# A graph network's first layer: its products placed behind every third group of edge counts in place of every second

## The chip, the cores and the metric

The kernel runs on one core of one Trainium2 chip, as one program in one launch. The metric is the device time of one execution in microseconds (us); below it is given as the median of 14 runs, and one more execution was profiled.

## What is computed

Four graph layers run one after the other over 6250 nodes with 128 features and 206250 edges (src, dst, weight), sorted by dst. Ahead of each stands a layer norm with ReLU, and each adds its result to x. Cut to what matters here, layer 0 and the shape of the rest:

```python
h = relu(layernorm(x))
neighbor = segment_sum(edge_weight[:, None] * h[src], dst, 6250)       # layer 0
x = x + leaky_relu(neighbor @ W1.T + b1 + (h * neighbor) @ W2.T + b2, 0.2)
h = relu(layernorm(x))
x = x + graph_norm_layer(h, segment_sum(h[src], dst) / degree)         # layer 1
x = x + clique_layer(relu(layernorm(x)))                               # layer 2: means of x_clique rows, one linear map
x = x + gru_layer(relu(layernorm(x)))                                  # layer 3: sums of messages, GRU gates, one linear map
```

## The kernel before

Instead of gathering rows by edge, the kernel builds dense matrices. The nodes are cut into 49 blocks of 128. For every destination node it counts, by source node, how many edges there are (`cnt`, small integers) and how large the sum of their weights is (`edge_w`). Layer 0 multiplies by `edge_w` as soon as it is there. The counts go to DRAM, straight (`cnt_d`) and turned by DMA transposes (`cntT_d`), and layers 1 to 3 read them in a second stage (`dense`, line 1023), which the change doesn't touch.

**Strips.** The first stage takes 25 strips of 256 destination nodes (two blocks; the last strip has one). In a strip, two nodes share the 128 partitions as two halves of 64 (`WN` = 2, `H` = 64): a partition holds one edge of a node. Four such pairs of nodes (`PW` = 4) make one **count**, so a strip has 32 counts, numbered 0 to 31 below, and the last strip 16.

**A count** (`count`, line 769) is 24 bf16 matmuls on PE (line 784) of one-hot matrices: `s_hot` (which node within a source block) as weights, `k_hot` (which block, and the same times the three parts of the edge's weight) as moving operand. They write a PSUM tile `pK` of two banks. ACT then copies it out twice: cast to 8-bit integers into `cnt` (line 793), and a copy into `edge_w` (line 791). The pool `banks` has three such tiles (line 606), and the tag `pK` is shared: the transposes `pt` and `pv` and the products `po` and `pf` named below each take one of the three in turn as well.

**One-hots** (`one_hots`, line 750) are made by DVE for four counts at a time (`TW` = 16): `s_hot` (line 762) and `k_hot` (lines 764 and 765). There are two sets. At the first count of a group of four, the set for the next group is put into DVE's queue; it overwrites the set of the group before.

**The products of layer 0** (`layer0`, line 813) for strip k are made while strip k+1 is counted: 49 source blocks, for each of them one fp32 matmul by each half of the partitions, into `pB` and `pM` (line 821; each runs as two instructions, so a source block is two steps of a pair). `layer0` is a generator: each call of `next(before)` issues one **visit** of some source blocks and stops. Before the change there are 16 visits, each of three source blocks but for the last with four. After the last visit ACT and DVE add `pB` and `pM` into `agg` (lines 829 and 830), and `finish0` (line 845) is queued as the **ends** of that strip.

**Ends and keys** come at fixed places too. `finish0` is a generator that is visited before the counts 2, 6, 10, 14, 18, 22 and 30 of the following strip (`END_AT`, piece by piece; four counts are a piece): the transposes `pt` of h (line 842) with DVE's product `inter` (line 851), then the products `po` (lines 858 and 859) with the sums and statistics on DVE, then the norm's steps on ACT and DVE, a second `pt` before count 22 that ACT copies to `ht`, and `pf` (line 879) before count 30. The keys of the next strip are prepared by `prepare` (line 667), begun behind count 27 of the strip before and visited before the counts 2, 10, 14, 22 and 26 (`EDGES_AT`): offsets on DVE (lines 683 to 705, then 714 to 705), indirect fetches of edges by POOL (line 642), the split of the weights in three on POOL (lines 586 to 589), and before count 26 five transposes `pv` on PE (line 739), which ACT copies out as `keys` and `by_edge` (line 744).

The whole order is written by hand: the stage stands under a manual schedule, and what is issued first in Python stands first in each engine's queue. `strip` (line 940) lays it down. For each count: a new set of one-hots if a group begins; the visits for ends and keys if the count is the third of its piece; the count; a visit of the products if the count's number is odd (lines 962 and 963); and after the last count of a piece the DMA transposes of `turn`, on SP's queue. So a visit for ends and keys always stands right behind a visit of the products.

Of the kernel before, what the change touches and what calls it, by code (L numbers as in the profile page):

```python
# [464 lines left out]
WN = 2  # L465
H = P // WN
SB = 2
SW = SB * P
STRIPS = [(k, min(SB, NB - k * SB)) for k in range(-(-NB // SB))]
NS = len(STRIPS)  # L470
TW = 16
TI = 2
PW = 4
# [26 lines left out]
def fast(ctx: ExitStack, tc: tile.TileContext, a: dict, out: bass.AP, flag: bass.AP):  # L500
# [41 lines left out]
    def flat(t):  # L542
        return t.rearrange("p b f -> p (b f)")
# [55 lines left out]
    with ExitStack() as bx:  # L599
# [150 lines left out]
        def one_hots(by_edge, t0):  # L750

            of = slice(t0 // TI, t0 // TI + tq)
            keys, parts = (t[:, of, :, None, :] for t in by_edge)

            def at(i, n):
                return keys[:, :, i].to_broadcast([P, tq, n, TI])

            def count_up(n):
                return iota[:, None, :n, :].to_broadcast([P, tq, n, TI])

            s_hot = hot.tile([P, tq, P, TI], BF16, name="s_hot")
            nc.vector.tensor_tensor(s_hot, count_up(P), at(0, P), op=ALU.is_equal)  # L762
            k_hot = hot.tile([P, tq, 4, NBP, TI], BF16, name="k_hot")
            nc.vector.tensor_tensor(k_hot[:, :, 0], count_up(NBP), at(1, NBP), op=ALU.is_equal)  # L764
            nc.vector.tensor_tensor(k_hot[:, :, 1:, :NB], k_hot[:, :, :1, :NB].to_broadcast([P, tq, 3, NB, TI]),  # L765
                                    parts.to_broadcast([P, tq, 3, NB, TI]), op=ALU.mult)
            return s_hot, k_hot

        def count(w0, hots, cnt, edge_w):

            s_hot, k_hot = hots

            pk = banks.tile([P, WN, 512], F32, name="pK")
            for i in range(PW):
                (u, t), o = divmod(w0 % TW + i, TI), 2 * NBP * i
                for j in (0, 2, 3):
                    for h in range(WN):
                        r = slice(h * H, (h + 1) * H)
                        if j:
                            to, rhs = slice(o + NBP, o + NBP + NB), k_hot[r, u, j, :NB, t]  # L780
                        else:
                            both = k_hot[r, u, :2, :, t].rearrange("p j b -> p (j b)")
                            to, rhs = slice(o, o + NBP + NB), both[:, : NBP + NB]
                        nc.tensor.matmul(pk[:, h, to], s_hot[r, u, :, t], rhs, start=j == 0,  # L784
                                         stop=True, skip_group_check=True)
            by_block = pk[:, :, : 2 * PW * NBP].rearrange("p h (i c b) -> p c b i h", c=2, b=NBP)
            n0, nn = w0 * WN, PW * WN
            pairs = flat(cnt).bitcast(U8).rearrange("p (b n e) -> p b e n", n=P, e=2)
            for j, m in enumerate((pairs[:, :, :, n0 % P : n0 % P + nn], edge_w[:, :, n0 : n0 + nn])):
                if j:  # L790
                    nc.scalar.copy(m.rearrange("p b (i h) -> p b i h", h=WN), by_block[:, 1, :NB])  # L791
                else:
                    nc.scalar.copy(m.rearrange("p b e (i h) -> p b e i h", h=WN),  # L793
                                   by_block[:, 0].rearrange("p (b e) i h -> p b e i h", e=2))

        def turn():


            kept = None
            for g in range(NQB):  # L800
                c, i = CHUNK_OF[g]
                for q in range(0, NPR, KP):
                    tt = turned.tile([P, KP, P], U16, name="tt")
                    nc.sync.dma_start_transpose(tt, cnt_d[c, :, i, q * P : (q + KP) * P])
                    if kept:
                        nc.sync.dma_start(*kept)
                    kept = cntT_d[:, g, q * P : (q + KP) * P], flat(tt)
                    yield
            nc.sync.dma_start(*kept)

        turns0 = SW // (WN * PW * 2)

        def layer0(k, nb, edge_w):

            g, w = k * SB, nb * P
            pl = [psum.tile([P, 512], F32, name=n) for n in ("pB", "pM")]
            for i in range(turns0):
                for s in range(i * NB // turns0, (i + 1) * NB // turns0):
                    for h in range(WN):
                        r = slice(h * H, (h + 1) * H)  # L820
                        nc.tensor.matmul(pl[h][:, :w], h0[r, s, :], edge_w[r, s, :w], start=s == 0,  # L821
                                         stop=s == NB - 1)
                if i + 1 < turns0:
                    yield
            if k == NS - 1:
                ends.append(pl)
                return
            agg = work.tile([P, SW], F32, name="agg")
            nc.scalar.copy(agg[:, :w], pl[0][:, :w])
            nc.vector.tensor_add(agg[:, :w], agg[:, :w], pl[1][:, :w])  # L830
            ends.append(finish0(g, nb, agg))
# [99 lines left out]
        before, ends, turns, edges = iter(()), [], turn(), prepare(1)  # L931
# [8 lines left out]
        def strip(k, nb):  # L940
            nonlocal before, edges, by_edge, hots
            edge_w = edge[k % 2].tile([P, NB, SW], F32, name="edge_w")
            end = ends.pop() if ends else iter(())
            last, piece, following = nb * P // WN, 0, None
            for w0 in range(0, last, PW):
                if w0 % TW == 0:
                    now, t1 = hots, w0 + TW
                    if t1 < last:
                        hots = one_hots(by_edge, t1)
                    elif following:  # L950
                        hots = one_hots(following, 0)
                if w0 // PW % PT == PT // 2:
                    if piece in END_AT:
                        next(end, None)
                    if piece in (EDGES_AT if k else FIRST_AT):
                        following = next(edges, None)
                if w0 // PW % 2 and piece in (NORMS_AT[k] if k < 2 else ()):
                    next(norming, None)
                if w0 * WN % P == 0:
                    cnt = cnts.tile([P, NPR, P], U16, name="cnt")  # L960
                count(w0, now, cnt, edge_w)
                if k and w0 // PW % 2:
                    next(before, None)
                g, w1 = k * SB + w0 * WN // P, w0 + PW
                if w1 * WN % P == 0:
                    c, i = CHUNK_OF[g]
                    nc.sync.dma_start(cnt_d[c, :, i, :], flat(cnt))
                if w1 % (PW * PT) and w1 < last:
                    continue
                if piece == NEXT_AT and k + 2 < NS:  # L970
                    edges = prepare(k + 2)
                    next(edges)
                for _ in range(TURN_AT.count(piece) if k else 0):
                    next(turns, None)
                piece += 1
            by_edge = following
            for _ in before:
                next(end, None)
            for _ in end:
                pass  # L980
            before = layer0(k, nb, edge_w)

        def found_all():

# [5 lines left out]
            nc.vector.tensor_copy(flag, p_all)  # L990

        strip(*STRIPS[0])
        nc.vector.tensor_add(b12, b12, b2)
        for k, nb in STRIPS[1:-1]:
            strip(k, nb)
        total = found_all()
        next(total)
        strip(*STRIPS[-1])
        end = ends.pop()
        pt = banks.tile([P, WN, 512], F32, name="pt", tag="pK")  # L1000
# [525 lines left out]
def gnn_kernel(tc: tile.TileContext, a: dict, out: bass.AP):  # L1526
    nc = tc.nc
    with tc.tile_pool(name="flag", bufs=1) as keep:
        flag = keep.tile([1, 1], I32, name="flag")
        fast(tc, a, out, flag)  # L1530
        found = nc.values_load(flag[0:1, 0:1], min_val=0, max_val=2 * E,
                               skip_runtime_bounds_check_because="a count of edges, each at most twice")
        with tc.If(found != E):
            general(tc, a, out)
# [48 lines left out]
```

## Time and profile before

| | |
|---|---|
| median of 14 runs | 1844.3 us (1842.52 to 1845.45) |
| the profiled execution | 1843.03 us |
| its span, first to last instruction | 1841.2 us |
| granted TensorE clock, mean | 0.990 |
| first strip begins to count at | 31.3 us |
| second strip | 71.4 us |
| third strip | 111.5 us |
| the last strip (25th) | 955.9 us |
| the dense layers begin at | 1001 us |
| DVE's busy time per strip (529.6 to 567.8) | 33.9 of 38.2 us |
| ACT's busy time per strip (the same) | 28.8 of 38.2 us |

Engines are PE (matmul), PEld (weight load, beside PE), DVE, ACT, POOL and SP, which issues DMAs. Times are us from the start of the span. In a row of the timeline stand start, duration, engine, line, operation, output<-input with their shapes and the number of instructions merged (x48); where the engine stood idle before, the idle time and what ended it follow in brackets. Matmuls are pipelined: a row's duration is longer than the distance to the next start, and it is the distance that PE's queue pays. Shown durations are rounded to 0.01 us. In the list of waits stand the waiting engine and line, what it waited for, the total, the number of waits and the longest.

### The profile page before, as it was taken

The page shows a single profiled execution, that of the slowest core. Times are in us where ns is not written, and L with a number is a line of the kernel's source. Part 1 is how long each engine was busy: PE and PEld are TensorE (multiplying, and loading weights), DVE is VectorE, ACT ScalarE, POOL GpSimd, SP SyncE. Part 2 cuts the span into 40 slices and gives each one's busy share as a digit, 9 for nine tenths or more (in the row PEclk, how much of TensorE's full clock was granted, in tenths as well). Part 3 has the DMA queues.
Part 4 walks back from the last instruction along what each step waited for, and adds up shares of the span by engine and source line. Part 5 has one row for each costly group of instructions (what it writes and reads, how often), then busy time and mean ns, then how long its engine had stood idle before and what let it go on. Part 6 is the DMA issues. An engine that isn't in the chain of part 4 may idle for free. (4 is left out here: it accounts for less than half of the span.)

```text
span 1841.2 us, 65339 instructions
## 1 busy us (share of the span) xinstructions
PE 1777.7 (97%) x28191; PEld 1511.7 (82%) x28191; DVE 1392.3 (76%) x2946; ACT 1203.7 (65%) x2835; POOL 474.0 (26%) x431
## 2 busy tenths in 40 slices
PE   2799999999999999999999999999999999999997
PEld 2698888888888888888888888888888877787776
DVE  7888888888888888888886777777777854444543
ACT  5777777777777777777774777777556653443442
POOL 2433334333334333343323012111122200000000
PEclk9799999999999999999999999999999999999999
DMA  4255554544535555454214555554555544344442
GB/s 106 57 123 119 127 124 100 140 117 124 121 100 133 112 124 121 100 132 114 83 56 152 163 172 170 166 152 125 147 148 149 154 134 152 109 149 137 133 131 61
DMA packets 262514, 231.73 MB, mean 126 GB/s; under 512 B 101518, under 2 KB 246424, under 8 KB 262215
## 3 DMA queue, kind: packets, MB, share of 16 engines
q1 hardware_dynamic: 253415, 210.67, 42.6%
q0 software_dynamic: 8800, 16.78, 3.3%
q8 instruction: 223, 3.65, 0.8%
q14 instruction: 76, 0.62, 0.1%
HBM read 130.37 MB, written 76.54 MB: 112 GB/s over the span
## 5 line engine op out<-in xcount | busy, mean ns | idle before, releaser
L821 PE MATMUL pB<-edge_w,h 64*128 64x256 f32 (+1 forms) x2450 | 613.1, 385 | 1.0 <-issue 0.7
L821 PE MATMUL pM<-edge_w,h 64*128 64x256 f32 (+1 forms) x2450 | 613.2, 385 | 0.0
L1086 PE MATMUL acc<-wide,parts 128*128 128x512 f32 (+2 forms) x2548 | 574.1, 383 | 2.7 <-DVE wide L1064 1.3
L1086 PEld LDWEIGHTS acc<-wide,parts 128*128 128x128 f32 x2548 | 460.3, 188 | 100.8 <-issue 10.5
L793 ACT CAST cnt<-pK 128x400 uint8<-128x400 f32 x784 | 397.6, 507 | 192.8 <-PE pK L784 175.7
L821 PEld LDWEIGHTS pB<-edge_w,h 64*128 64x128 f32 x2450 | 422.2, 187 | 34.9 <-issue 1.3
L784 PEld LDWEIGHTS <-s_hot 64*128 64x128 bf16 x18816 | 379.4, 95 | 70.9 <-issue 18.0
L821 PEld LDWEIGHTS pM<-edge_w,h 64*128 64x128 f32 x2450 | 422.0, 187 | 0.4 <-DVE flag L990 0.2
L784 PE MATMUL pK<-k_hot,s_hot 64*128 64x49 bf16 (+1 forms) x18816 | 396.6, 192 | 25.3 <-ACT edge_w L791 11.4
L791 ACT COPY edge_w<-pK 128x392 f32<-128x392 f32 x784 | 400.8, 511 | 0.0
L765 DVE TENSOR_TENSOR k_hot<-k_hot,by_edge 128x2352 bf16<-128x2352 bf16 x196 | 272.3, 1389 | 8.5
L762 DVE TENSOR_TENSOR s_hot<-iota,keys 128x2048 bf16<-128x2048 bf16 x196 | 239.3, 1221 | 43.5 <-PE pK L784 41.5
L1064 DVE TENSOR_SCALAR_CACHE_REDUCE wide<-ring 128x512 fp32r<-128x512 uint8 (+2 forms) x325 | 193.3, 650 | 25.4 <-issue 15.9
L1062 ACT ACTIVATE wide<-ring 128x512 fp32r<-128x512 uint8 (+2 forms) x312 | 184.7, 595 | 24.3 <-ACT wide L1062 19.6
L642 POOL DMA_INDIRECT dst<-in_dst,off_i x50 | 84.8, 1696 | 378.9 <-DVE node L705 369.4
L1056 ACT CAST wide<-ring 128x1024 fp32r<-128x1024 uint8 (+3 forms) x130 | 120.7, 957 | 71.0 <-PE acc L1086 68.2
L1055 DVE CAST wide<-ring 128x1536 fp32r<-128x1536 uint8 (+2 forms) x130 | 119.6, 945 | 53.3 <-PE acc L1086 41.2
L1086 PE MATMUL acc<-wide,q_parts 128*128 128x512 f32 (+2 forms) x650 | 157.4, 392 | 1.2 <-DVE wide L1041 1.2
L1086 PEld LDWEIGHTS acc<-wide,q_parts 128*128 128x128 f32 x650 | 115.6, 188 | 28.2 <-DVE wide L1041 2.9
L764 DVE TENSOR_TENSOR k_hot<-iota,keys 128x800 bf16<-128x800 bf16 x196 | 125.9, 642 | 0.0
L1427 POOL DMA_DIRECT2D out<-x x12 | 10.2, 851 | 322.9 <-DVE x L1424 293.1
L642 POOL DMA_INDIRECT src<-in_src,off_i x50 | 78.0, 1561 | 15.2 <-issue 15.2
(246 smaller groups left out, 1610.6 us busy)
## 6 DMA issues: line engine op xcount, KB each, us to landing
ring<-cnt_d SPq DMA_DIRECT2D x110, 640.0 KB, 4.5
cnt_d<-cnt SPq DMA_DIRECT2D x49, 800.0 KB, 4.5
cntT_d<-tt SPq DMA_DIRECT2D x125, 160.0 KB, 3.5
ring<-cntT_d SPq DMA_DIRECT2D x60, 320.0 KB, 3.1
ring<-cnt_d SPq DMA_DIRECT2D x10, 480.0 KB, 3.5
ring<-cnt_d SPq DMA_DIRECT2D x10, 320.0 KB
h<-in_x SPq DMA_DIRECT2D x12, 256.0 KB, 4.4
xs<-in_x SPq DMA_DIRECT2D x24, 128.0 KB, 3.8
```

Of the source, the lines that this page charges most:

```text
L642: nc.gpsimd.indirect_dma_start(out=t, out_offset=None, in_=col[name], in_offset=bass.IndirectOffsetOnAxis(ap=idx, axis=0))
L762: nc.vector.tensor_tensor(s_hot, count_up(P), at(0, P), op=ALU.is_equal)
L764: nc.vector.tensor_tensor(k_hot[:, :, 0], count_up(NBP), at(1, NBP), op=ALU.is_equal)
L765: nc.vector.tensor_tensor(k_hot[:, :, 1:, :NB], k_hot[:, :, :1, :NB].to_broadcast([P, tq, 3, NB, TI]), parts.to_broadcast([P, tq, 3, NB, T ...
L784: nc.tensor.matmul(pk[:, h, to], s_hot[r, u, :, t], rhs, start=j == 0, stop=True, skip_group_check=True)
L791: nc.scalar.copy(m.rearrange("p b (i h) -> p b i h", h=WN), by_block[:, 1, :NB])
L793: nc.scalar.copy(m.rearrange("p b e (i h) -> p b e i h", h=WN), by_block[:, 0].rearrange("p (b e) i h -> p b e i h", e=2))
L821: nc.tensor.matmul(pl[h][:, :w], h0[r, s, :], edge_w[r, s, :w], start=s == 0, stop=s == NB - 1)
L1056: nc.scalar.copy(to[:, 3:ks], of[:, 3:ks])
L1062: one = nc.scalar.activation(to[:, k], of[:, k], AF.Copy, accum_out=total)
L1064: one = nc.vector.tensor_scalar(to[:, k], of[:, k], 1.0, None, op0=ALU.mult, op1=ALU.add, accum_out=total)
L1086: nc.tensor.matmul(acc[:, : nb * P], parts[:, s, j, :], rhs, start=s + j == 0, stop=s == end and j == 1)
```

## The change

The products get a visit after every third count of a strip in place of every second, and after the last count. The number of visits is set to match: 32 counts over 3, rounded up, are 11, so that a visit has four or five source blocks (4, 4, 5, 4, 5, 4, 5, 4, 5, 4, 5). They stand behind the counts 2, 5, 8, 11, 14, 17, 20, 23, 26, 29 and 31. In the last strip of 16 counts there are six (2, 5, 8, 11, 14, 15) for the strip before it, and the other five follow behind the counts. The products of the last strip itself keep 16 pieces. All instructions stay, and their sizes; ends and keys stay before the counts at which they stood. Which visits of ends and keys stand right behind products does change: those before the counts 6, 18 and 30 do, the others stand between two counts.

```diff
-        turns0 = SW // (WN * PW * 2)
-
-        def layer0(k, nb, edge_w):
+        every = 3
+        turns0 = -(-SW // (WN * PW) // every)
+
+        def layer0(k, nb, edge_w, turns0):
...
                 count(w0, now, cnt, edge_w)
-                if k and w0 // PW % 2:
+                if k and (w0 // PW % every == every - 1 or w0 + PW == last):
                     next(before, None)
...
-            before = layer0(k, nb, edge_w)
+            before = layer0(k, nb, edge_w, turns0 if k < NS - 1 else SW // (WN * PW * 2))
```

In this text a line number is that of the kernel before; from line 812 on the changed kernel's are one higher.

## Prediction

> **What bounds the kernel now.** I read the page first, then busy time by stretches, then who waited for whom, then single stretches of the timeline.
>
> The busy line of the page, and the table of stretches for the third strip (starts at 111.5) and for one in the middle (columns: stretch; its length; busy us of PE, PEld, DVE, ACT, POOL; granted clock; DMA):
>
> ```profile
> PE 1777.7 (97%) x28191; PEld 1511.7 (82%) x28191; DVE 1392.3 (76%) x2946; ACT 1203.7 (65%) x2835; POOL 474.0 (26%) x431
> ```
> ```profile
> 111.50:149.70 38.20, 38.20 (x993) 33.84 (x991) 33.47 (x60) 28.82 (x71) 14.67 (x12) 1.00 0.45 118
> 529.60:567.80 38.20, 38.20 (x992) 33.84 (x990) 33.86 (x61) 28.81 (x72) 14.53 (x13) 1.00 0.48 119
> ```
>
> PE is busy in all of a strip's 38.20 us; DVE in 33.9, ACT in 28.8. From 111 to 950 the list of waits has for PE only:
>
> ```profile
> PE pK L784 <- issue: 1.6, 2, 0.9
> PE pB L821 <- issue: 0.7, 2, 0.4
> ```
>
> So in layer 0 time is what PE's queue holds, in order, and any new wait of PE is lost. Twenty-two strips (the 3rd to the 24th) run alike, 38.21 us each but for four of 39.0 to 39.3.
>
> **What a visit costs.** One pair of counts and one visit, on PE:
>
> ```profile
> 543.91 0.95 PE L784 MATMUL pK<-k_hot,s_hot 64*128 64x99 bf16 x48
> 544.70 0.46 PE L821 MATMUL pB<-edge_w,h 64*128 64x256 f32 x1
> ...
> 545.00 0.38 PE L821 MATMUL pB<-edge_w,h 64*128 64x256 f32 x1
> ...
> 545.22 0.38 PE L821 MATMUL pB<-edge_w,h 64*128 64x256 f32 x1
> ...
> 546.08 0.31 PE L784 MATMUL pK<-k_hot,s_hot 64*128 64x99 bf16 x8
> ```
>
> Two counts take 0.79 (0.40 each). The first products of a visit take 0.30 until the next start, all others 0.216, so a visit costs 0.08 beside its products, and a source block (two such steps) 0.432. Blocks stay 49 per strip; visits fall from 16 to 11: 5 x 0.08 = **-0.41 per strip**. A visit becomes 1.81 (four blocks) or 2.24 (five). That is the whole gain on PE, except that the transposes of line 739 now follow a count and no longer a product (0.31 until they start, against 0.21 within a visit): -0.09.
>
> **What the counts then meet.** A count writes one of three buffers in turn (tag pK), shared with the transposes (pt, pv) and products (po, pf) of the visits for ends and keys. In the second strip, where ACT is late, the rule can be read (ACT, then PE):
>
> ```profile
> 77.38 0.48 ACT L791 COPY edge_w<-pK 128x392 f32<-128x392 f32 x1
> ...
> 78.14 0.50 ACT L791 COPY edge_w<-pK 128x392 f32<-128x392 f32 x1
> ```
> ```profile
> 77.91 0.57 PE L784 MATMUL pK<-k_hot,s_hot 64*128 64x99 bf16 x24 [0.74 <-ACT edge_w L791]
> 78.69 0.57 PE L784 MATMUL pK<-k_hot,s_hot 64*128 64x99 bf16 x24 [0.20 <-ACT edge_w L791]
> ```
>
> 77.38 + 0.48 = 77.86 and 78.14 + 0.50 = 78.64: each count starts 0.05 after a copy ends; counted through, it is the copy of the count three before it. How late that copy is with ACT at rest, for the pair at 543.91:
>
> ```profile
> 544.51 0.49 ACT L793 CAST cnt<-pK 128x400 uint8<-128x400 f32 x1 [0.51 <-PE pK L784]
> 544.90 0.49 ACT L791 COPY edge_w<-pK 128x392 f32<-128x392 f32 x1
> ```
>
> Cast 0.60 after the count's start, copy done at 545.39, so its buffer comes back 1.53 after the count began. Two counts and a visit take 2.2: hidden today, since every visit for ends or keys stands right behind a product visit (counts 2, 6, 10 ... behind counts 1, 5, 9 ...). With thirds, products stand behind counts 2, 5, 8, ..., 29 and 31. The visits before counts 6 and 30 still follow one. Three that use a buffer do not: before count 2 (pt), 22 (pt), 26 (pv).
>
> T is us from count 0.
>
> - Count 2 comes third after count 0 (0, 1, pt, 2). It arrives at 0.80 + 0.12 (four transposes, as from 520.93 to 521.05) = 0.92. ACT first copies agg (533.79 to 534.17, count 0 at 533.59), casts at 534.24, has copied at 535.12: buffer back at T = 1.53 + 0.05 = 1.58. **+0.66**. The transposes lose 0.30 there today (1.22 from 535.77 to 536.98, less 0.80 of counts, less 0.12) in the order of PE's two halves; that falls under this wait: **-0.30**.
> - Count 4 needs pt's buffer, freed by DVE's product L851. DVE today:
>
> ```profile
> 536.27 1.38 DVE L765 TENSOR_TENSOR k_hot<-k_hot,by_edge 128x2352 bf16<-128x2352 bf16 x1
> 537.58 0.41 DVE L851 TENSOR_TENSOR inter<-agg,pt 128x256 f32<-128x256 f32 x1
> ```
>
>   Its chain (agg, one-hots, L851) starts with the strip and is not moved: done at 537.99, T = 4.40, plus 0.05. PE arrives at 1.58 + 0.40 + 1.81 + 0.40 = 4.19: **+0.26** (today it arrives at 4.67).
> - Count 23 comes third after count 21 (21, pt, 22, 23): arrives 0.92 after count 21's start, may start after 1.53: **+0.62**.
> - Count 26 comes third after count 24 (24, 25, pv, 26): 0.80 + 0.385 (pv, 563.70 to 564.09) = 1.19 against 1.53: +0.35. But pv also waits for POOL:
>
> ```profile
> 547.77 0.14 DVE L705 TENSOR_SCALAR node<-f_node 128x1 f32<-128x1 f32 x1
> ```
> ```profile
> 562.63 0.63 POOL L589 TENSOR_TENSOR vals<-rest,vals 128x128 bf16<-128x128 f32 x1
> ```
>
>   POOL's fetches and splits end at 563.27, 15.4 after L705, whose place on DVE hardly moves (T = 14.4): vals come at 29.8. PE reaches pv at T = 29.1 (with the waits above; today 30.1), its last transpose can start at 29.85, count 26 at 30.0. **+0.49** in all.
>
> Sum per strip: -0.41 - 0.09 - 0.30 + 0.66 + 0.26 + 0.62 + 0.49 = **+1.23**, so 39.44.
>
> One-hots: DVE may start a set when the group of four counts two back has been counted, and needs 3.13 (551.52 to 554.65) after 0.20 of latency. Between the end of count 15 and count 20 there are four counts and one four-block visit, 1.6 + 1.81 = 3.41: 0.2 + 3.13 + 0.05 = 3.38 just fits. Elsewhere there is a second visit, or line 858's products (1.09), as cover; the margin at count 8 is 0.6. If that cover goes, PE waits once per strip. ACT has 0.77 x 3 = 2.3 of copies per 3.2 and the same other work; SP's and POOL's transfers keep their places and get a longer strip.
>
> The other strips: no product visits in the first. The second has no ends, and ACT, with the norms' work, is behind in half of it; -0.4 + 0.5 (pv) + a bound of 1 either way: +0.3. The last (16 counts, one block): the waits at counts 2 and 4 less two visits, +0.66 + 0.26 - 0.30 - 0.16 = +0.5. The dense layers after 1001 us aren't touched.
>
> 22 x 1.23 + 0.3 + 0.5 = 27.9. The profiled execution took 1843.0 (span 1841.2 and 1.8 around it): 1843.0 + 27.9 = 1870.9. The median of the runs is 1844.3, 1.3 above the profiled one: **1872**.
>
> **Bounds.** Low: no wait at count 4, pv only by its bank, -0.80 + 0.62 + 0.62 + 0.35 = +0.79, x 22 = 17.4, 1862. High: pv 0.3 later and the one-hots of count 20 late by 0.36 (L573 and L575, which stand ahead of them, 550.86 to 551.22), +1.9, x 22 = 42, 1886.
>
> **A rule that speaks against the change.** Short waits left the clock alone here: PE had 1.8 us of gaps in the second strip's first half, single ones up to 0.74, at clock 1.00; the clock had been 0.50 in a stretch after one wait of 4.9 us (47.2 to 52.1).
>
> ```profile
> 74.20:91.80 17.60, 15.82 (x418) 13.77 (x414) 15.01 (x49) 15.11 (x41) 6.04 (x5) 1.00 0.24 38
> 50.30:57.10 6.80, 4.27 (x131) 3.91 (x132) 4.66 (x10) 6.79 (x19) 4.92 (x4) 0.50 0.34 129
> ```
>
> The Trainium skill ("TensorE: Matmul & The Clock Gate", "A second HAM failure mode: psum-queue depth-cycling") warns that PE, idling briefly between groups of matmuls as it cycles PSUM banks, can swing between full and half clock. By it, with that page's window of 3.4 us at half clock once a strip, an estimate would add 22 x 1.7 = 37 us. The sum goes by the row: nothing.
>
> **Rivals.**
> 1. *Waits as worked out*: 1872, own range 1862 to 1882. 70%.
> 2. *DVE or POOL fall behind too*: the one-hots' margin of 0.03 goes, or pv comes later: 1882 to 1895. For: 33.9 of 38.2 us DVE busy. Against: the strip grows by 1.2, which gives DVE time. 15%.
> 3. *Waits partly hidden*: one of the two waits for ACT does not come; +0.3 to +0.7 per strip, 1850 to 1862. 7%.
> 4. *Faster*: the count behind pt or pv finds its buffer free, so that only the visits' starts change: 23 x (-0.41 - 0.09) = -11.5, 1833. The place is the buffer of the count two before pt; it decides if that comes back within 0.92 of the count's start. Against: 1.53 in the rows. 5%.
> 5. *Gain and waits cancel*, within 0.2% (about what a measurement of this kernel can tell from no change): 3%. That the edit does nothing is out: on PE the same instructions stand in another order, products behind every third count.
>
> Faster 0.05 (case 4), same 0.03 (5), slower 0.92. The range 1858 to 1886 takes case 1, some half of 2 and the top of 3.
>
> **What would show it.** Right: strips of 39.4; PE waits in L784 with ACT edge_w as releaser, some 1.3 us a strip, before the third and the 24th count; a smaller one for DVE inter, one at pv for POOL vals; first products of a visit still 0.30, 11 per strip; clock 1.00. Wrong: strips under 38.2 with no wait at those counts (case 4); L784 waiting for k_hot L765 at count 20 (case 2); a clock below 1.00.

## The result, and the profile after

| | before | after |
|---|---|---|
| median | 1844.3 us (28 runs, 1842.38 to 1845.45) | 1865.98 us (6 runs, 1864.92 to 1867.37) |
| ratio, 95% interval | | 1.0118 [1.0108, 1.0128] |
| profiled execution, its span | 1843.03, 1841.2 us | 1866.88, 1865.1 us |
| second, third, last strip begin | 71.4, 111.5, 955.9 us | 71.3, 112.8, 979.2 us |
| a strip with no other pause | 38.21 us | 39.29 us |

Slower by 1.2%, as predicted (1872, with a range of 1858 to 1886). On two occasions the kernel before itself took some 1868 us instead of some 1845, for reasons that stay open, so the kernels run on one of those occasions are compared only with one another.

The busy line of the page after, and the table of stretches for two strips (fourth and fourteenth; columns as before):

```profile
PE 1773.2 (95%) x28191; PEld 1514.5 (81%) x28191; DVE 1405.6 (75%) x2946; ACT 1190.5 (64%) x2835; POOL 474.5 (25%) x431
```
```profile
152.61:191.89 39.28, 38.10 (x991) 34.03 (x989) 34.14 (x60) 28.24 (x71) 14.98 (x13) 1.00 0.56 122
546.15:585.45 39.30, 38.16 (x991) 34.22 (x989) 34.32 (x60) 28.24 (x71) 14.60 (x12) 1.00 0.49 114
```

PE had no gap in 38.20 us before; now it is busy for 38.1 of 39.3, with ACT and DVE about as busy as before. The clock is still 1.00. The list of waits of PE from 112 to 975 names what came in:

```profile
PE pK L784 <- ACT edge_w L791: 22.5, 60, 0.7
PE pv L739 <- POOL vals L589: 1.4, 3, 0.5
PE pK L784 <- issue: 0.3, 1, 0.3
PE pB L822 <- issue: 0.2, 1, 0.2
```

Sixty waits for ACT's copy where there was none. (The list counts idle time after the modelled end of the matmul before, so its figures are lower than the distances between starts, which are what PE loses.) They stand before the counts 2, 23 and 26, three to a strip, except in strips where PE was late there anyway. A fourth wait, before count 4, is too short for the list: PE loses 0.25 there, but the idle time left of it is about 0.1. It shows in the starts. DVE and PE in the fourteenth strip (count 0 at 546.15):

```profile
550.13 0.41 DVE L852 TENSOR_TENSOR inter<-agg,pt 128x256 f32<-128x256 f32 x1
```
```profile
547.73 0.57 PE L784 MATMUL pK<-k_hot,s_hot 64*128 64x99 bf16 x24 [0.46 <-ACT edge_w L791]
549.94 1.63 PE L784 MATMUL pK<-k_hot,s_hot 64*128 64x99 bf16 x72
```

The first row of PE is count 2, the second holds the counts 3, 4 and 5. DVE is done with the buffer of `pt` at 550.13 + 0.41 = 550.54, and count 4 starts at 550.60; over the 22 strips it starts 0.05 behind the end of that row (median), as predicted.

The wait before count 23 in the timeline, PE and then ACT:

```profile
570.75 0.55 PE L784 MATMUL pK<-k_hot,s_hot 64*128 64x99 bf16 x24
571.14 0.31 PE L843 MATMUL pt<-f_ident,h 64*128 64x64 f32 x4
571.29 0.56 PE L784 MATMUL pK<-k_hot,s_hot 64*128 64x99 bf16 x24
572.27 0.57 PE L784 MATMUL pK<-k_hot,s_hot 64*128 64x99 bf16 x24 [0.42 <-ACT edge_w L791]
```
```profile
571.34 0.49 ACT L793 CAST cnt<-pK 128x400 uint8<-128x400 f32 x1 [0.89 <-PE pK L784]
571.73 0.49 ACT L791 COPY edge_w<-pK 128x392 f32<-128x392 f32 x1
```

Count 21 starts at 570.75, the transposes follow, then count 22; ACT has copied count 21 at 571.73 + 0.49 = 572.22, and count 23 starts 0.05 later, 1.52 after count 21. Without the wait it would have started 0.40 behind count 22, at 571.69: 0.58 lost. ACT had stood idle for 0.89 before it: it isn't ACT's load that delays, but the two operations in a row that free the buffer, behind a count of 0.40.

### The profile page after: what moved, and what is told of

Same layout as the page of the kernel before. It is cut to its first block, busy times and chain, and to the rows that moved or that the text cites. A ratio compares the mean times of both kernels' runs of the same rounds, so it can differ in the third digit from the quotient of the medians.

```text
span 1865.1 us, 65362 instructions
## 1 busy us (share of the span) xinstructions
PE 1773.2 (95%) x28191; PEld 1514.5 (81%) x28191; DVE 1405.6 (75%) x2946; ACT 1190.5 (64%) x2835; POOL 474.5 (25%) x431
## 4 chain that ended last, share of the span: by engine, by line
PE 80%; DVE 9%; ACT 3%; issue 3%; DMA 2%; POOL 2%; POOLq 0%; DVEq 0%; ACTq 0%
PE acc L1087 35%; PE pB L822 22%; PE pK L784 13%; DVE k_hot L765 2%; DVE s_hot L762 2%; ACT cnt L793 1%; DMA wgt<-in_edge_weight,off_i 1%; PE pA L1231 1%; PE pM L822 1%; ACT edge_w L791 1%; DVE k_hot L764 1%; PE pf L880 1%; PE po L859 1%; PE pM L1378 1%; PE pA L1423 1%
## 5 line engine op out<-in xcount | busy, mean ns | idle before, releaser
L822 PE MATMUL pB<-edge_w,h 64*128 64x256 f32 (+1 forms) x2450 | 583.5, 381 | 0.4 <-ACT agg L830 0.3
L822 PE MATMUL pM<-edge_w,h 64*128 64x256 f32 (+1 forms) x2450 | 583.2, 381 | 0.0
L793 ACT CAST cnt<-pK 128x400 uint8<-128x400 f32 x784 | 405.7, 517 | 238.2 <-PE pK L784 236.2
L822 PEld LDWEIGHTS pB<-edge_w,h 64*128 64x128 f32 x2450 | 430.9, 187 | 35.8 <-ACT agg L830 0.4
L784 PEld LDWEIGHTS <-s_hot 64*128 64x128 bf16 x18816 | 369.3, 95 | 98.4 <-issue 51.5
L784 PE MATMUL pK<-k_hot,s_hot 64*128 64x49 bf16 (+1 forms) x18816 | 386.0, 192 | 53.0 <-ACT edge_w L791 38.5
L822 PEld LDWEIGHTS pM<-edge_w,h 64*128 64x128 f32 x2450 | 430.8, 187 | 1.2 <-DVE flag L991 0.2
L791 ACT COPY edge_w<-pK 128x392 f32<-128x392 f32 x784 | 409.0, 522 | 0.0
L762 DVE TENSOR_TENSOR s_hot<-iota,keys 128x2048 bf16<-128x2048 bf16 x196 | 251.5, 1283 | 39.7 <-PE pK L784 37.5
L1406 DVE SCALAR_TENSOR_TENSOR wb<-pT,f_b_hh,wb 128x512 f32<-128x512 f32 (+1 forms) x12 | 8.9, 740 | 91.1 <-PE pT L1403 91.1
```

## Experiments

Theory A is that of the prediction: a count finds its buffer occupied when it comes third after a count that began less than 1.53 us earlier; such a wait is PE's, and lost. Rival B: ACT's work as a whole sets the strip, and a wait taken away at one place comes back at another.

### One and three visits put back behind products

```diff
+        VISIT_AT = {0: 3, 5: 21, 6: 27}      # one visit: {5: 21}
...
-                if w0 // PW % PT == PT // 2:
+                if w0 // PW == (VISIT_AT if k else {}).get(piece, PT * piece + PT // 2):
```

The first two runs, on the first of the two occasions (before: 1868.98 us):

**p5_behind**. 

> The changed kernel, with one visit moved: the ends and keys that stand before count 22 stand before count 21, right behind the products of count 20. Theory A (a count waits for the copy of the count three buffers back, and does so where no visit of the products lies between): the wait of 0.58 us at count 23 goes in each of 22 strips, and nothing else moves: 1866.0 - 13 = 1853 us, strips of 38.7. Theory B (what costs is the cadence itself, three counts in a row and longer visits, wherever ends and keys stand): within 2 us of 1866.

**three_behind**. 

> The changed kernel with all three visits that use a buffer between counts moved behind a visit of the products: from before count 2 to before 3, from 22 to 21, from 26 to 27. Theory A: the waits for ACT's copies at counts 2 (0.63), 23 (0.58) and 26 (0.26) go. Count 4 now waits for the one-hots, whose chain on DVE starts behind the sums of layer 0: it can start at T = 4.11 in place of 4.46, so 0.35 is won at the strip's beginning and not 0.88. Per strip -0.35 - 0.58 - 0.26 - 0.1 = -1.25 to -1.3, 22 strips: 1866.0 - 28 = 1838 us (1834 to 1844). Theory B: 1866.

They took 1979.02 and 1948.98 us: neither theory's number, since 114 and 95 pauses of PE came in that have no releaser (in the lists of waits, releaser `issue`). The changed kernel itself had to be run beside them, and both were run again with it (before: 1867.6 us):

**after_again**. 

> The changed kernel, nothing else, as a yardstick beside the other three on the same chip. Theory A (PE waits for the copy of the count three buffers back, 1.72 us a strip in all): 1866 where the kernel before takes 1844, ratio 1.012. Theory S (the pauses in which PE waits for nothing that the profile shows, and the half clock after them, come with the chip and not with a kernel): if the kernel before is again near 1869 here, this one is well above 1890 too, with some 50 such pauses in layer 0. Theory K (they come with the kernels of the first four runs): no such pauses here whatever the chip.

**p5_again**. 

> The changed kernel with one visit (ends, before count 22) put one count earlier, so that it stands right behind products. Theory A: the wait of 0.58 us before count 23 goes in all 22 strips, those before counts 2, 4 and 26 stay: 22 x 0.58 = 12.8 us less than the changed kernel on this chip (1853 beside 1866). Theory B (ACT's work as a whole sets the strip, and the wait shows up at another place): the same as the changed kernel. Theory K: slower than the changed kernel by 100 us again, with pauses of PE that have no releaser.

**three_again**. 

> The changed kernel with all three such visits put right behind products (before counts 3, 21 and 27). Theory A: no wait on edge_w by PE in layer 0 any more but in the second strip; a wait of up to 0.4 us for one-hots at count 4 in its place; 22 x (1.72 - 0.4) = 29 us less than the changed kernel on this chip, some 1838 beside 1866, that is 6 us less than the kernel before. Theory B: the same as the changed kernel. Theory K: 80 us slower than the changed kernel again, with pauses that have no releaser.

Measured 2011.12 us (ratio to before 1.0767 [1.0745, 1.079]), 1983.07 and 1967.75. So the pauses don't belong to the moved visits (theory K falls; S had put some 50 pauses, and there are 132), and moving them gains 28 and 43 us even there. The waits of PE in layer 0 can be read beside the pauses; after_again (112 to 1121), p5_again (112 to 1096), three_again (112 to 1070):

```profile
PE pK L784 <- issue: 66.8, 132, 0.7
PE pK L784 <- ACT edge_w L791: 24.0, 66, 0.7
```
```profile
PE pK L784 <- issue: 61.7, 118, 0.7
PE pK L784 <- ACT edge_w L791: 14.7, 44, 0.7
```
```profile
PE pK L784 <- issue: 57.2, 117, 1.4
PE pK L784 <- DVE k_hot L765: 9.4, 22, 0.5
PE pB L822 <- issue: 0.4, 1, 0.4
```

One visit moved takes 22 of 66 waits away, three take all. From the starts, the medians over the strips of after_again are 0.63 before count 2, 0.25 before 4, 0.58 before 23 and 0.26 before 26, those of the changed kernel's first profile to 0.01; p5_again keeps the first two and the last at 0.63, 0.25 and 0.26 and has nothing before 23. The totals went further than A said (28 us where 12.8 were expected, 43 for 29): the pauses, 66.8, 61.7 and 57.6 us in these lists, change as well, so the totals carry more than the waits.

**three_third**, the same kernel, when the kernel before took 1845.65 us. 

> The changed kernel with the three visits put right behind products (before counts 3, 21 and 27), once more, for conditions in which the kernel before takes some 1845 and PE has only single pauses without a releaser. Theory A: no wait of PE for edge_w in layer 0 but in the second strip; a wait of up to 0.4 us for one-hots at count 4 in its place; strips of 37.9 to 38.1 us, 1837 to 1842 in all, ratio 0.996 to 0.999 to the kernel before. Theory B (ACT's work as a whole sets the strip): strips of 39.3 as in the changed kernel, 1866. If the kernel before takes 1868 again: 1950 to 1970 with some 75 to 115 pauses, as twice before.

1851.5 us, ratio 1.0029 [1.0017, 1.0041]: 14.5 less than the changed kernel's 1866, with undisturbed strips of 38.29 against 39.29. B is out. A's 1837 to 1842 was missed by 10, and the list of waits (112 to 955) says where:

```profile
PE pK L784 <- DVE k_hot L765: 9.3, 22, 0.5
PE pK L784 <- issue: 2.4, 6, 0.6
PE pB L822 <- issue: 0.4, 1, 0.4
```

No wait for ACT, but one in every strip for one-hots. PE and DVE at that place:

```profile
502.55 0.28 PE L843 MATMUL pt<-f_ident,h 64*128 64x64 f32 x4
502.66 0.56 PE L784 MATMUL pK<-k_hot,s_hot 64*128 64x99 bf16 x24
503.65 0.72 PE L784 MATMUL pK<-k_hot,s_hot 64*128 64x99 bf16 x32 [0.43 <-DVE k_hot L765]
```
```profile
502.21 1.38 DVE L765 TENSOR_TENSOR k_hot<-k_hot,by_edge 128x2352 bf16<-128x2352 bf16 x1
```

Count 4 could start at 502.66 + 0.40 = 503.06; the one-hots are there at 503.59. It loses 0.59, where at most 0.4 were expected: once the waits before it are gone, PE is at count 4 earlier, and DVE's set is late. Single pauses (2.8 us in the list), a second strip of 42.42 us (40.08 in the kernel before, 41.51 in the changed one) and 889.2 us for the last strip and the dense layers (885.3 and 885.8) come on top; why these two are longer wasn't followed up.

### The size of the wait: one more cast of 0.52

The cast into `cnt` (line 793) is done twice for one count, 21 or 22, in the 22 strips from the third to the 24th.

```diff
-                else:
+                    continue
+                for _ in range(casts):
                     nc.scalar.copy(m.rearrange("p b e (i h) -> p b e i h", h=WN),
...
-                count(w0, now, cnt, edge_w)
+                count(w0, now, cnt, edge_w, 2 if k > 1 and w0 // PW == 21 else 1)
```

**cast_twice_21**. 

> The changed kernel, with ACT's cast of count 21 done twice from the third strip on (the same values again, 0.38 to 0.39 us more of ACT in each of 23 strips). Theory A: the copy of count 21 ends that much later, and count 23, the third after it by buffers, starts that much later: +0.38 x 22 = +8.5, 1874.5 us. Theory B, or ACT's slack hiding it (ACT is busy 28.7 of 39.3 us): 1866.

**cast_twice_22**. 

> The same second cast, of count 22 in place of 21: the same work more on ACT. Theory A: the buffer of count 22 is next used by count 25, with a visit of the products between; nothing waits for it, so 1866 within 2 us. A theory by which ACT's total work sets the time: the same as for count 21, 1874.5.

Both were run beside p5_behind, so only the difference counts: 2024.39 and 2008.95 us. The place before count 23, with the second cast at 21 (ACT, PE) and at 22 (PE):

```profile
524.39 1.02 ACT L794 CAST cnt<-pK 128x400 uint8<-128x400 f32 x2 [1.44 <-PE pK L784]
525.30 0.49 ACT L791 COPY edge_w<-pK 128x392 f32<-128x392 f32 x1
```
```profile
525.84 0.57 PE L784 MATMUL pK<-k_hot,s_hot 64*128 64x99 bf16 x24 [0.94 <-ACT edge_w L791]
```
```profile
514.92 0.57 PE L784 MATMUL pK<-k_hot,s_hot 64*128 64x99 bf16 x24 [0.42 <-ACT edge_w L791]
```

The median of the wait, from the starts, is 1.10 with the cast at 21 and 0.58 with the cast at 22: the same work on ACT, but only ahead of the copy that count 23 needs does it cost PE anything, and there all of it: 0.52, the distance by which the second cast moves the copy (525.30 - 524.39 = 0.91, against 571.73 - 571.34 = 0.39 with one). Theory A had the place right and the size too low, at 0.38. 22 x 0.52 = 11.4; the totals differ by 15.4, and the rest isn't accounted for. The wait at its place settles which copy is waited for.

### Visits behind a count, with products every second count

```diff
+        VISIT_AT = {0: 3, 1: 7, 2: 11, 3: 15, 4: 19, 5: 23, 6: 27, 7: 31}
...
-                if w0 // PW % PT == PT // 2:
+                if w0 // PW == (VISIT_AT if k else {}).get(piece, PT * piece + PT // 2):
```

**half_mid** (run beside after_again). 

> The kernel before (products behind every second count) with every visit for ends and keys put one count later, so that none of them follows products directly. Theory A: what costs is that the next count comes third after a count within 1.53 us; here products stand between (count 2, visit, count 3, products, count 4), so no wait: within 4 us of the kernel before (1840 to 1848 beside 1844). Theory V (a visit of transposes that follows a count and not products costs by itself, some 0.5 us each, whatever the buffers): 8 x 0.5 x 22 = 88 us more.

1889.75 us, 22 above the kernel before on that occasion, where A put at most 4 (ratio 1.0105 [1.0081, 1.0128]). Not V's 88, and in layer 0 from the third strip on no wait for any engine, as A says; but 65 pauses without a releaser:

```profile
PE pK L784 <- issue: 24.5, 65, 0.7
PE pB L821 <- issue: 0.4, 1, 0.4
```

In most strips they are three, 0.35, 0.67 and 0.56 from start to start, some 1.5 in all; the strips' usual 39.9 less 1.5 is 38.4, near the 38.21 of the kernel before. How many pauses the kernel before has on that occasion isn't known, so the 22 us settle nothing by themselves.

### The pauses without a releaser

**before_again** and **after_plain** were meant for the pauses.

```diff
-                fetch(src[:, half], "src", off_i)
-                fetch(wgt[:, half], "edge_weight", off_i)
+                for t, name in ((src, "src"), (wgt, "edge_weight")):
+                    if k:
+                        nc.sync.dma_start(t[:, half], a[name][: P * H].rearrange("(p j) -> p j", j=H))
+                    else:
+                        fetch(t[:, half], name, off_i)
```

> The kernel before, nothing else, for its trace in the conditions of the last runs. It took 1868 there, 24 more than in its profiled execution. Theory G (PE is short of instructions while GpSimd issues the four gathers of sources and weights, 17 to 22 us into each strip, and counts use up instructions ten times as fast as products do): about 1.0 us of pauses per strip, all at the counts that run at that time, shorter than the changed kernel's 3.3 because only two counts come between products. Theory C (a chip that is slower throughout): the 24 us are spread over the whole layer or lie in the dense layers. If the conditions are those of the first runs: 1844 and four pauses only.

> The changed kernel with the four gathers of sources and weights (GpSimd, L642) replaced by plain loads of fixed edges on SyncE's queue, for all strips but the first: it leaves out which edges these are, and so counts other sources and weights. Theory G: the pauses 18.8 to 22.2 us into each strip and the half clock after them go, strips are 39.3 again with the four waits of 0.63, 0.25, 0.58 and 0.26 in them, 1866 to 1885 in conditions in which the changed kernel takes 2011 (the pauses at the gather of lines, some 0.5 us a strip, may stay). Theory P (the place in the program, or the chip, makes PE short of instructions, whatever GpSimd does): 2011 again.

They met the other conditions (before: 1845.97): 1846.26 and 1864.58 us (ratio 1.0102 [1.0085, 1.0119]), neither with more than single pauses. So the question whether the gathers cause them wasn't put. What after_plain shows is that the waits don't depend on the gathers (112 to 975; its lines are three higher):

```profile
PE pK L787 <- ACT edge_w L794: 23.8, 66, 0.5
PE pB L825 <- issue: 0.2, 1, 0.2
```

### A version that beats both

```diff
+            first = 6 if k < NS - 1 else NB // turns0
+            cuts = [0] + [first + i * (NB - first) // (turns0 - 1) for i in range(turns0)]
             for i in range(turns0):
-                for s in range(i * NB // turns0, (i + 1) * NB // turns0):
+                for s in range(cuts[i], cuts[i + 1]):
```

**three_six**: three_third with this. 

> The three visits right behind products, as in three_third, and the first visit of products in a strip takes six blocks instead of four (the other ten share 43). Count 4 is then reached 2 x 0.43 = 0.86 us later, and its one-hots, 0.59 us late in three_third, are there. Theory A: no wait of PE for edge_w or k_hot but single ones, strips of 38.29 - 0.59 = 37.7 us, 0.5 less than in the kernel before; 22 x 0.59 = 13 us less than three_third, some 1839, ratio 0.996. Theory D (VectorE's sequence of one-hots sets the strip): the wait comes back before count 8 or 20, and the strips stay at 38.3, 1851. If the kernel before takes 1868: 1940 to 1960, with the pauses without a releaser.

1839.98 us (1837.77 to 1841.77) beside 1846.0: ratio 0.9964 [0.995, 0.9977]. The waits from 112 to 965, and two of its strips:

```profile
PE pK L784 <- issue: 2.4, 5, 1.2
PE pv L739 <- POOL vals L589: 0.6, 2, 0.4
PE pM L824 <- issue: 0.2, 1, 0.2
```
```profile
303.44:341.08 37.64, 37.49 (x989) 34.88 (x987) 33.95 (x60) 28.33 (x71) 16.20 (x13) 1.00 0.57 127
455.47:493.10 37.63, 37.57 (x989) 34.95 (x987) 33.87 (x60) 28.34 (x71) 15.68 (x12) 1.00 0.58 123
```

Neither ACT nor the one-hots are waited for, and the strips without a pause fell by 0.66 to 37.63 (D is out). The others have up to 0.6 more, one of them 1.35; the mean is 37.97, and for most of this no releaser is named. So fewer visits of products do pay, once nothing that takes a buffer stands between two counts and the first visit covers DVE: 0.4% against the kernel before. An undisturbed strip is 0.58 shorter than there; 0.39 of it is PE's time in products (22.74 to 22.35 from the starts, medians), most of the rest its time in counts. The kernel before with the same moves and its 16 visits wasn't run, so what the moves are worth by themselves stays open.

## Why the prediction was right, step by step

| step, us per strip | predicted | measured |
|---|---|---|
| five visits fewer (PE's time in products) | -0.41 | -0.46 (22.74 to 22.28) |
| wait before count 2 | +0.66 | +0.63 |
| wait before count 4 | +0.26 | +0.25 |
| wait before count 23 | +0.62 | +0.58 |
| pv and count 26 | +0.49 | +0.26 |
| first transposes no longer mixed with counts, pv behind a count | -0.39 | -0.18 (what remains of the sum) |
| sum | +1.23 | +1.08 |

The first four steps held to 0.05. **pv** was mis-sized. The step let PE wait for POOL: "POOL's fetches and splits end at 563.27, 15.4 after L705", read from one strip alone. Over the 22 strips the split ended between 27.5 and 31.1 us into the strip in the kernel before and between 27.8 and 30.2 after; PE came at 29.2 (29.1 was worked out), and had a wait for it that the list takes in three strips only (1.4 us in all). What is left is the wait for the buffer alone, 0.26, which the prediction had at 0.35 for its lower bound. The one-hots of count 20, a margin of 0.03, were in time.

**The last row.** Of its two terms the -0.09 came to nothing. Behind products the transposes `pv` had started 0.10 late, and the -0.46 of the first row holds that gain; but they start late behind a count as well, since count 25 now lasts 0.50 in place of 0.39 (medians). This miss of +0.21 and the -0.23 at pv nearly cancel: that the sum came within 0.15 is in part luck.

**The rest.** 22 x 1.08 = 23.8. The second strip went from 40.08 to 41.51, +1.4 where +0.3 was put: its count 4 waits 3.1 us for ACT's copy of count 1, which stands in ACT's queue behind a step of the norm that waits for DVE (3.01 us, line 568). The last strip and the dense layers give +0.6 (predicted +0.5). Four strips of before were 0.8 to 1.1 longer by pauses without a releaser; after, less of that shows, -1.8 in all. 23.8 + 1.4 + 0.6 - 1.8 = 24.0; the spans differ by 23.9. Against the forecast's 27.9 that is 22 x 0.15 = 3.3 less from the strips, 1.8 less from the pauses and 1.2 more from the other strips. The other 2 us between 1872 and 1866 lie in the profiled executions: before, it is 1.3 below the median, and after 0.9 above.

**The clock.** It stayed at 1.00 (mean from 112.84 to 979.25) with four waits of up to 0.63 in each strip, so the estimate by the Trainium skill ("TensorE: Matmul & The Clock Gate", "A second HAM failure mode: psum-queue depth-cycling") of 37 us did not come; here the row decided. Rival 4's condition, the buffer back within 0.92, is met by no strip: 1.52 after count 21 in the rows above.

## What to carry to other kernels

Before work is moved away from between two users of a rotating buffer, work out for each user how long its buffer is out (here 1.53 us for a count of 0.40) and what stands between it and the third user after it; taking out five fixed costs of 0.08 brought four waits of 0.25 to 0.63. A rotation with three buffers and a short user needs a long piece of work in every three; where a fourth user is slipped in, put it next to that piece. And read a duration that decides a wait over all repetitions, not over one.

## What was not expected

**PE can pause without waiting for anything that the profile shows.** On the second of the two occasions the changed kernel took 143 us more than the kernel before (2011.12 - 1867.6), against 21.7 otherwise. In after_again pauses like these come in every strip from the third on (PE, then POOL, at the same time):

```profile
321.18 0.26 PE L784 MATMUL pK<-k_hot,s_hot 64*128 64x99 bf16 x5 [0.46 <-issue]
321.93 0.29 PE L784 MATMUL pK<-k_hot,s_hot 64*128 64x99 bf16 x6 [0.49 <-issue]
322.70 0.26 PE L784 MATMUL pK<-k_hot,s_hot 64*128 64x99 bf16 x5 [0.48 <-issue]
```
```profile
319.92 0.94 POOL L642 DMA_INDIRECT wgt<-in_edge_weight,off_i  x1 [0.30 <-issue]
321.17 0.94 POOL L642 DMA_INDIRECT src<-in_src,off_i  x1 [0.30 <-issue]
322.42 1.57 POOL L642 DMA_INDIRECT wgt<-in_edge_weight,off_i  x1 [0.30 <-issue]
```

Five or six matmuls, then nothing for half a microsecond, waiting for no semaphore. In all four kernels of that occasion, and in each of these strips, such pauses lie between 18.6 and 23.1 us into the strip (for half_mid's ninth strip 23.6), while POOL issues the gathers of sources and weights (from 16.6 to some 23). In after_again a sixth pause follows 37.7 to 40.0 us into the strip, 0.8 to 1.0 behind the start of POOL's gather `line`; it is there in the 21 strips (third to 23rd) that have this gather, and missing in the 24th, which has none. What they cost stands in the table of stretches (before, in, and after it):

```profile
301.40:320.20 18.80, 18.24 (x504) 16.35 (x501) 16.53 (x34) 12.81 (x32) 5.36 (x4) 1.00 0.43 102
320.20:324.40 4.20, 1.57 (x39) 0.85 (x31) 2.42 (x3) 0.88 (x2) 3.18 (x3) 1.00 0.44 146
324.40:327.80 3.40, 3.37 (x24) 2.76 (x26) 0.68 (x1) 2.43 (x6) 0.71 (x2) 0.58 0.74 203
```

In 4.2 us PE is busy for 1.57, and then the granted clock is down for 3.4 us: a pair of products takes 0.40 instead of 0.216. The strip takes 45.3 us instead of 39.3, 4.7 of the difference in counts and 1.3 in products. The same page of the Trainium skill (section "HAM oscillation — how this bites in real kernels") tells of a clock that is lost again and again, each time after an idle stretch of more than 3.4 us. This trace differs: here no single pause was longer than 0.71 us, and PE was busy for 37% of the 4.2 us. Waits of 0.63 spread over a strip did not have that effect. Nor did a longer one in the second strip of the changed kernel's first profile, with a wait of 2.95 us and PE busy for only 1.17 of 4.20 us:

```profile
74.30:78.50 4.20, 1.17 (x50) 0.94 (x47) 4.03 (x19) 2.55 (x8) 1.21 (x1) 1.00 0.87 121
78.50:82.00 3.50, 3.17 (x88) 2.81 (x88) 3.28 (x14) 2.84 (x9) 0.53 (x1) 1.00 0.05 14
```

So the length of an idle time alone doesn't say what becomes of the clock, and what does these runs don't settle. The Trainium skill ("Runtime: NRT & Kernel Launch", "Instruction fetch mechanics") has the fetch of instructions mostly hidden. If the pauses are PE short of instructions, it was not hidden here; no run shows whether they are.

What stays open: what makes these conditions (one of the two chips that showed them gave 1846.0 for the kernel before at another time, so it isn't the chip alone), and whether the gathers cause the pauses or only coincide with them. Kernels with three counts in a row had 117 to 132 pauses on the second occasion and the one with two in a row 65. That would fit the rates, since a count issues 48 instructions (24 matmuls, each with its weight load) in 0.40 us and a visit 32 to 40 in 1.8 to 2.2, so some seven times as many per us (the ten times in the expectation of before_again is too high); but it wasn't tried by itself.
